# Storing two samples per transfer: one 8 KB run per partition against two rows of 4 KB

## The chip, the cores and the metric

The kernel runs on one core of a Trainium2 chip. The metric is the device time of one execution in microseconds, as the median over runs. Lower is better.

## The reference

There are 128 samples `x[b]` of 128 channels by 1024 time steps in float32, a subject number in 0..7 for each sample, and a table of 8 weight matrices of 128 by 128. Each sample is multiplied by the weights of its subject, and the product is added to it:

```python
w = weights[subjects]
out = jnp.einsum('bct,bcd->bdt', x, w)
x = x + out
```

The input x and the output are 67.1 MB each.

## The kernel before

The 128 samples are taken in 64 groups of two (`G = 2`). A group lives in one of 23 SBUF buffers (`SLOTS = 23`) of 128 partitions by 2 x 1024 floats, so 8 KB per partition and 1 MB per group. The buffers are used in turn. The sum is written over the sample in its buffer, and the buffer is then stored.

- SP issues all the big loads, one of 512 KB per sample, through the helper `transfer` (L53). Each reads runs of 16 KB from HBM (four channels of a sample are contiguous there) and writes one row of 4 KB into each partition. In the first turn SP lets only a few groups be in flight (it waits for the load of three groups earlier); in later turns it waits on `s_store` until the buffer's previous contents have been stored.
- POOL copies the weights of a sample's subject out of `w_all` into one of four buffers (L158).
- PE waits for the load, and multiplies: two matmuls of 512 columns per sample into PSUM (L164), which the profile shows as four records.
- DVE adds the product to the sample, in place (L174), and counts `s_added`.
- ACT waits on `s_added` for both samples of a group and issues one store of 1 MB (also through `transfer`, L53). `s_store` of the buffer tells when it has landed.

Nothing is planned or reordered: each engine runs its own list in the order of the program, and semaphores tie them together. Loads go through SP's DMA queue (q1 in the profile), stores through ACT's (q10). Both queues are served by the same 16 DMA engines. `transfer` builds the DMA instruction itself from both access patterns, so that the two sides may have differently shaped runs; `dma_start` is the language's usual call.

Of the kernel before, what the change touches and what calls it, by code (L numbers as in the profile page):

```python
# [1 line left out]

# [4 lines left out]

F32 = mybir.dt.float32
I32 = mybir.dt.int32
ALU = mybir.AluOpType


G = 2

N = 512  # L30

SLOTS = 23

W_SLOTS = 4
P_SLOTS = 4
DMA = 16

LEAD = 3

IDLE = 3  # L40

ROWS = 4
QUEUES = {mybir.EngineType.SP: "qSPDynamicHW", mybir.EngineType.Activation: "qActDynamicHW"}


def transfer(nc, engine, out, in_):

    later, nc._always_lower_symbolic_ap = nc._always_lower_symbolic_ap, False  # L50
    ins, outs = engine.lower_ap_dma(in_), engine.lower_ap_dma(out)
    nc._always_lower_symbolic_ap = later
    return engine.add_instruction(  # L53
        mybir.InstDMACopy(
            name=nc.get_next_instruction_name(),
            engine=engine.engine,
            ins=ins,
            outs=outs,
            mode="Copy",
            cce_op=ALU.bypass,  # L60
            queue=QUEUES[engine.engine],
        )
    )


@with_exitstack
def kernel(
    ctx: ExitStack,
    tc: tile.TileContext,
    x: bass.AP,  # L70
    subjects: bass.AP,
    weights: bass.AP,
    out: bass.AP,
):
    nc = tc.nc
    B, C, T = x.shape
    S, _, D = weights.shape
    NT = B // G

    def sbuf(name, *shape, dtype=F32):  # L80
        return ctx.enter_context(nc.sbuf_tensor(name, list(shape), dtype)).ap()

    given, near, wrap, index = (
        sbuf(name, 1, B, dtype=I32) for name in ("given", "near", "wrap", "index")
    )
    w_all = sbuf("w_all", C, S, D)
    ws = [sbuf(f"w{i}", C, 1, D) for i in range(W_SLOTS)]
    zeros = sbuf("zeros", C, N)
    xs = [sbuf(f"x{i}", C, G, T) for i in range(SLOTS)]
    ps = [  # L90
        ctx.enter_context(nc.psum_tensor(f"ps{i}", [D, T], F32)).ap() for i in range(P_SLOTS)
    ]

    s_given = tc.alloc_semaphore("s_given")
    s_wall = tc.alloc_semaphore("s_wall")
    s_index = tc.alloc_semaphore("s_index")
    s_zeros = tc.alloc_semaphore("s_zeros")
    s_copied = tc.alloc_semaphore("s_copied")
    s_product = tc.alloc_semaphore("s_product")
    s_added = tc.alloc_semaphore("s_added")  # L100
    s_load = [tc.alloc_semaphore(f"s_load{i}") for i in range(SLOTS)]
    s_store = [tc.alloc_semaphore(f"s_store{i}") for i in range(SLOTS)]

    with tc.tile_critical():  # L104

        nc.scalar.dma_start(given, subjects.rearrange("(o b) -> o b", o=1)).then_inc(s_given, DMA)

        nc.vector.memset(zeros, 0.0).then_inc(s_zeros, 1)  # L108
        nc.tensor.wait_ge(s_zeros, 1)
        for _ in range(IDLE):  # L110
            nc.tensor.matmul(  # L111
                ps[P_SLOTS - 1][:, :N], zeros[:, :D], zeros, start=True, stop=True
            )

        nc.vector.wait_ge(s_given, DMA)
        nc.vector.tensor_scalar(near, given, -S, S - 1, ALU.max, ALU.min).then_inc(s_index, 1)  # L118
        nc.vector.wait_ge(s_index, 1)
        nc.vector.tensor_scalar(wrap, near, 0, S, ALU.is_lt, ALU.mult).then_inc(s_index, 1)  # L120
        nc.vector.wait_ge(s_index, 2)
        nc.vector.tensor_tensor(index, near, wrap, ALU.add).then_inc(s_index, 1)  # L122
        nc.gpsimd.wait_ge(s_index, 3)

        nc.sync.dma_start(w_all, weights.rearrange("s c d -> c s d")).then_inc(s_wall, DMA)  # L127
        for i in range(NT):
            k, turn = i % SLOTS, i // SLOTS
            if turn:  # L130
                nc.sync.wait_ge(s_store[k], DMA * turn)
            elif i >= LEAD:
                nc.sync.wait_ge(s_load[k - LEAD], DMA * G)
            for g in range(G):
                transfer(
                    nc,
                    nc.sync,
                    xs[k][:, g, :],
                    x[i * G + g].rearrange("(a r) t -> a (r t)", r=ROWS),
                ).then_inc(s_load[k], DMA)  # L140

        nc.gpsimd.wait_ge(s_wall, DMA)
        for i in range(NT):
            k, turn = i % SLOTS, i // SLOTS
            nc.tensor.wait_ge(s_load[k], DMA * G * (turn + 1))
            for g in range(G):
                b = i * G + g
                s = nc.values_load(
                    index[0:1, b : b + 1],
                    engines=[mybir.EngineType.Pool],  # L150
                    min_val=0,
                    max_val=S - 1,
                    skip_runtime_bounds_check_because="the index is clamped on the chip above",
                )
                w, p = ws[b % W_SLOTS], ps[b % P_SLOTS]
                if b >= W_SLOTS:
                    nc.gpsimd.wait_ge(s_product, b - W_SLOTS + 1)
                nc.gpsimd.tensor_copy(w, w_all[:, bass.ds(s, 1), :]).then_inc(s_copied, 1)  # L158

                nc.tensor.wait_ge(s_copied, b + 1)  # L160
                if b >= P_SLOTS:
                    nc.tensor.wait_ge(s_added, b - P_SLOTS + 1)
                for t in range(0, T, N):
                    mm = nc.tensor.matmul(  # L164
                        p[:, t : t + N],
                        w[:, 0, :],
                        xs[k][:, g, t : t + N],
                        start=True,
                        stop=True,
                    )  # L170
                mm.then_inc(s_product, 1)

                nc.vector.wait_ge(s_product, b + 1)
                nc.vector.tensor_tensor(xs[k][:, g, :], p, xs[k][:, g, :], ALU.add).then_inc(  # L174
                    s_added, 1
                )
            nc.scalar.wait_ge(s_added, (i + 1) * G)
            transfer(
                nc,
                nc.scalar,  # L180
                out[i * G : (i + 1) * G].rearrange("g d t -> d g t"),
                xs[k].rearrange("d (o g) t -> d o (g t)", o=1),
            ).then_inc(s_store[k], DMA)


        for i in range(NT - SLOTS, NT):
            nc.sync.wait_ge(s_store[i % SLOTS], DMA * (i // SLOTS + 1))


# [1 line left out]
_INS = ["x", "itok_B_0_7", "L0_cond_weights"]  # L191
_OUTS = [((128, 128, 1024), "float32")]


# [20 lines left out]
```

## Time and profile before

| | us |
|---|---|
| median of 3 runs | 327.76 (327.57 to 328.29) |
| the profiled execution | 328.11 |
| its span, first to last instruction | 326.2 |
| PE busy | 239.9 (74%) |
| DVE busy | 157.9 (48%) |
| POOL busy | 37.8 (12%) |

The mean granted TensorE clock is 0.928. HBM traffic is 134.7 MB, 413 GB/s over the span. A line of the form `L164 PE MATMUL` names the line of the kernel, the engine and the operation. In a row of DMA queues stand the packets, the megabytes, and the time that the packets took as a share of the time of 16 engines. In rows of stages, a DMA share slightly above 1 means that the records of neighbouring packets overlap by a few ns.

### The profile page before, as it was taken

The page shows a single profiled execution, that of the slowest core. Times are in us where ns is not written, and L with a number is a line of the kernel's source. Part 1 is how long each engine was busy: PE and PEld are TensorE (multiplying, and loading weights), DVE is VectorE, ACT ScalarE, POOL GpSimd, SP SyncE. Part 2 cuts the span into 40 slices and gives each one's busy share as a digit, 9 for nine tenths or more (in the row PEclk, how much of TensorE's full clock was granted, in tenths as well). Part 3 has the DMA queues.
Part 4 walks back from the last instruction along what each step waited for, and adds up shares of the span by engine and source line. Part 5 has one row for each costly group of instructions (what it writes and reads, how often), then busy time and mean ns, then how long its engine had stood idle before and what let it go on. Part 6 is the DMA issues. An engine that isn't in the chain of part 4 may idle for free.

```text
span 326.2 us, 1941 instructions
## 1 busy us (share of the span) xinstructions
PE 239.9 (74%) x518; PEld 94.5 (29%) x518; DVE 157.9 (48%) x132; POOL 37.8 (12%) x132
## 2 busy tenths in 40 slices
PE   6999989889899998998898898898776866000000
PEld 2444333333333333333333333333232322000000
DVE  1676665565565555665565565666445446000000
POOL 1111111111111111111111111111111110000000
PEclk9999999999999999999999999999999999655555
DMA  7999999999999999999999999999999999999993
GB/s 259 418 415 424 423 420 425 421 430 422 427 424 423 422 426 421 426 424 427 425 425 422 425 427 420 425 424 422 424 432 430 420 422 424 428 424 428 424 428 163
DMA packets 16411, 134.86 MB, mean 413 GB/s; under 512 B 3089, under 2 KB 4114, under 8 KB 4114
## 3 DMA queue, kind: packets, MB, share of 16 engines
q1 hardware_dynamic: 7184, 67.64, 49.5%
q10 hardware_dynamic: 9218, 67.11, 49.1%
q8 instruction: 4, 0.07, 0.1%
q14 instruction: 5, 0.04, 0.0%
HBM read 67.63 MB, written 67.11 MB: 413 GB/s over the span
## 4 chain that ended last, share of the span: by engine, by line
DMA 45%; SPq 24%; another core or an unknown queue 13%; PE 1%; issue 1%; DVE 0%
DMA x<-in_x_dram 30%; SPq L53 23%; DMA out_dram<-x 15%; PE ps L164 1%; DVE x L174 0%; SPq L127 0%; SPq L211 0%; SPq L104 0%
## 5 line engine op out<-in xcount | busy, mean ns | idle before, releaser
L164 PE MATMUL ps<-x,w 128*128 128x512 f32 x512 | 234.7, 604 | 34.2 <-DMA x<-in_x_dram 34.1
L174 DVE TENSOR_TENSOR x<-ps,x 128x1024 f32<-128x1024 f32 x128 | 156.7, 1224 | 117.4 <-PE ps L164 117.4
L164 PEld LDWEIGHTS ps<-x,w 128*128 128x128 f32 x512 | 92.6, 189 | 176.7 <-issue 95.2
L158 POOL COPY w<-w_all 128x128 f32 x128 | 37.6, 294 | 228.3 <-PE ps L164 222.3
L111 PE MATMUL ps<-zeros 128*128 128x512 f32 x6 | 5.2, 1035 | 1.7 <-DVE zeros L108 1.7
L111 PEld LDWEIGHTS ps<-zeros 128*128 128x128 f32 x6 | 1.8, 328 | 3.7 <-issue 2.1
L108 DVE MEMSET zeros<- 128x512 f32 x1 | 0.5, 485 | 1.1 <-SPq L104 1.1
L118 DVE TENSOR_SCALAR near<-given 1x128 int32<-1x128 int32 x1 | 0.2, 215 | 0.6 <-DMA given<-in_itok_B_dram 0.6
L122 DVE CUSTOM_DVE_ANT_0 index<-near,wrap 1x256 uint16<-1x256 uint16 x1 | 0.3, 278 | 0.0
L120 DVE TENSOR_SCALAR wrap<-near 1x128 int32<-1x128 int32 x1 | 0.2, 215 | 0.0
L202 POOL MEMSET const-float32-0.0<- 128x1 f32 x1 | 0.1, 98 | 0.2 <-issue 0.2
L202 POOL MEMSET const-bfloat16-1.0<- 128x1 bf16 x1 | 0.1, 102 | 0.0
L202 POOL MEMSET const-uint8-127<- 128x1 uint8 x1 | 0.1, 102 | 0.0
L202 POOL MEMSET const-float32-1.0<- 128x1 f32 x1 | 0.1, 98 | 0.0
## 6 DMA issues: line engine op xcount, KB each, us to landing
x<-in_x_dram SPq DMA_DIRECT2D x128, 512.0 KB, 12.0
out_dram<-x ACTq DMA_DIRECT2D x64, 1024.0 KB, 40.6
w_all<-in_L_cond_weights_dram SPq DMA_DIRECT2D x1, 512.0 KB, 4.3
given<-in_itok_B_dram ACTq DMA_DIRECT2D x1, 0.5 KB
```

What stands on the lines that cost most here:

```text
L53: return engine.add_instruction(mybir.InstDMACopy(name=nc.get_next_instruction_name(), engine=engine.engine, ins=ins, outs=outs, mode="Cop ...
L108: nc.vector.memset(zeros, 0.0).then_inc(s_zeros, 1)
L111: nc.tensor.matmul(ps[P_SLOTS - 1][:, :N], zeros[:, :D], zeros, start=True, stop=True)
L118: nc.vector.tensor_scalar(near, given, -S, S - 1, ALU.max, ALU.min).then_inc(s_index, 1)
L120: nc.vector.tensor_scalar(wrap, near, 0, S, ALU.is_lt, ALU.mult).then_inc(s_index, 1)
L122: nc.vector.tensor_tensor(index, near, wrap, ALU.add).then_inc(s_index, 1)
L158: nc.gpsimd.tensor_copy(w, w_all[:, bass.ds(s, 1), :]).then_inc(s_copied, 1)
L164: mm = nc.tensor.matmul(p[:, t : t + N], w[:, 0, :], xs[k][:, g, t : t + N], start=True, stop=True,)
L174: nc.vector.tensor_tensor(xs[k][:, g, :], p, xs[k][:, g, :], ALU.add).then_inc(s_added, 1)
L202: nc = _bacc.Bacc("TRN2", target_bir_lowering=False, num_devices=1)
```

## The change

The store is issued with `dma_start` on the buffer as it is, 128 partitions by 2 rows by 1024 floats, where `transfer` had been given the two rows of a partition as one run of 2048 floats. The output side has the same shape in both: per partition two rows of 1024 floats in two samples. Loads are untouched and still go through `transfer`.

```diff
             nc.scalar.wait_ge(s_added, (i + 1) * G)
-            transfer(
-                nc,
-                nc.scalar,
-                out[i * G : (i + 1) * G].rearrange("g d t -> d g t"),
-                xs[k].rearrange("d (o g) t -> d o (g t)", o=1),
+            nc.scalar.dma_start(
+                out[i * G : (i + 1) * G].rearrange("g d t -> d g t"), xs[k]
             ).then_inc(s_store[k], DMA)
```

## The prediction

> **What bounds the kernel now.** I read the page first: the 40 slices, the DMA queues, the groups. Then I asked for sums over stages and for the DMA queues inside single stages.
>
> ```profile
> span 326.2 us, 1941 instructions
> ...
> PE   6999989889899998998898898898776866000000
> ...
> DMA  7999999999999999999999999999999999999993
> GB/s 259 418 415 424 423 420 425 421 430 422 427 424 423 422 426 421 426 424 427 425 425 422 425 427 420 425 424 422 424 432 430 420 422 424 428 424 428 424 428 163
> ...
> q1 hardware_dynamic: 7184, 67.64, 49.5%
> q10 hardware_dynamic: 9218, 67.11, 49.1%
> ...
> x<-in_x_dram SPq DMA_DIRECT2D x128, 512.0 KB, 12.0
> out_dram<-x ACTq DMA_DIRECT2D x64, 1024.0 KB, 40.6
> ```
>
> From the second slice to the last but one the 16 DMA engines are 90% busy or more, at about 424 GB/s; no compute engine is as full. The two queues share that time almost equally. The load queue (q1) has 128 loads of 32 pieces of 16 KB, the 1024 pieces of 512 B of w_all, and the semaphore writes: 128 x (32 + 16) + 1024 + 16 = 7184. The store queue (q10) has 64 x (128 + 16) + 2 = 9218, so a store today is 128 pieces of 8 KB and 16 semaphore writes. PE stops at about 277 us (slice 35 on); the rest is stores alone. So the end is set by the work of the DMA engines, not by a wait of PE, DVE or POOL.
>
> Next, the stages (us; busy time and count of PE, PEld, DVE, POOL; clock; DMA share; GB/s):
>
> ```profile
> 3.30:4.10 0.80, 0.80 (x2) 0.34 (x1) 0.00 (x0) 0.00 (x0) 1.00 1.09 330
> 5.00:16.00 11.00, 9.97 (x22) 4.05 (x21) 4.63 (x4) 2.34 (x8) 1.00 1.01 408
> 20.00:200.00 180.00, 161.81 (x354) 63.83 (x353) 107.86 (x89) 25.84 (x89) 1.00 1.01 424
> 225.00:270.00 45.00, 33.99 (x75) 13.31 (x74) 22.73 (x19) 5.25 (x18) 1.00 1.01 425
> 274.00:318.00 44.00, 1.74 (x5) 0.44 (x3) 2.45 (x2) 0.00 (x0) 0.56 1.01 426
> ```
>
> Row by row: w_all alone in 512 B pieces; 16 KB loads alone; loads and stores mixed while slots are free; mixed while loads wait for slots; stores alone. The queues within the long mixed stage (20 to 200 us), then within the stage of stores alone (274 to 318 us):
>
> ```profile
> DMA packets 8384, 76.39 MB, mean 424 GB/s; under 512 B 1859, under 2 KB 1859, under 8 KB 1859
> ...
> q1 hardware_dynamic: 4191, 45.82, 60.3%
> q10 hardware_dynamic: 4186, 30.49, 40.5%
> ```
>
> ```profile
> DMA packets 2574, 18.75 MB, mean 426 GB/s; under 512 B 285, under 2 KB 285, under 8 KB 285
> ```
>
> In the mixed stage the two queues move equally many packets (4191 and 4186), semaphore writes included, so an engine takes one from each in turn. That explains the bytes: two loads' turns of 16 KB and one semaphore against three stores' turns of which 8 in 9 carry 8 KB is 32 : 21.3 KB, 1.50; measured 45.82 / 30.49 = 1.50.
>
> [...]
>
> **The change part by part.** No compute instruction, wait, semaphore or buffer changes, and no order on any engine: ACT still issues 64 stores of 1 MB after the same waits on s_added, SP the same 128 loads. Only the view of the SBUF side changes: two rows of 4 KB per partition in place of one run of 8 KB. The HBM side was two rows of 4 KB, 512 KB apart, and remains so. The pieces on q10 go from 128 to 256 per store.
>
> *Cost of a piece, the dominating term.* With stores alone, 44 us x 16 engines = 704 engine-us for 2574 - 285 = 2289 pieces: 307.6 ns per 8 KB with its eighth of a semaphore write. That write is 9 ns in the trace's packet records, about 6 without the overlap with its neighbours, so 306.9 ns for the piece. With w_all alone, 330 GB/s is 16 x 512 / 330 = 24.8 ns for 512 B. A straight line through both gives 24.8 + 3584 x (306.9 - 24.8) / 7680 = 156.4 ns for 4 KB, 312.9 for two, against 306.9: 6.0 ns more for every 8 KB. Each engine has 64 x 128 / 16 = 512 such pairs, so +3.1 us. The lower bound comes from doubling at the other end. In the mixed stage 180 x 16 = 2880 engine-us, less 3722 stores at 307.6 ns (1145), less some 1400 load semaphores at 6 ns (8), leave 1727 for 2797 loads: 617 ns for 16 KB, just over twice 306.9. There, halving shows no cost: about -0.6 us if the same slope held to 4 KB[...]. [...] I take 2.4 us[...]; range -0.6 to +3.1.
>
> *Issue on ACT, nothing.* An issue now takes 546 ns at least and 3996 in the median because ACT waits for room; behind it stand only later stores. About 22.5 us from issue to landing at 426 GB/s are 9 stores in flight. If the queue has room for so many pieces, it will hold about half, some 5 MB, still over 11 us of work; that hides the doubled pieces. Without that cover, w_all shows the supply: 1024 pieces issued in 0.44 us and moved at 330 GB/s, 645 pieces per us, where stores alone need 426 GB/s / 4096 B = 104.
>
> *Shares of the queues, a moved stall.* Three load turns still bring 32 KB, three store turns now 3 x 16/17 x 4 = 11.3 KB: ratio 2.9 while both queues are full. Of about 424 GB/s, loads get some 315 and stores 109, in place of 255 and 169. Free slots run out sooner: 24.1 MB of slots, less 5.6 loaded by 16 us, less about 2 in flight, at 315 - 109 = 206 GB/s lasts 80 us, to about 96 us instead of about 210. After that SP's loads wait on s_store for most of the run, and the loads follow the stores at about 212 GB/s each. Both cover the same bytes, and a deep store queue stands behind every stall of SP, so the moved stall costs nothing by itself; loads end near 272 us again, with about 22 MB of stores left. PE's matmul records start 428 ns apart when PE does not wait, four per sample: 1.71 us per 512 KB, 306 GB/s. PE then runs back to back up to 96 us, a little behind the loads, and is late for nobody: stores want only 109 GB/s.
>
> *Sum.* The profiled execution took 328.11 us, its span 326.2, so 1.9 lie around it. Its own sum is 328.11 + 2.4 = 330.5; it stood 0.35 above the median of the runs, so I predict 327.76 + 2.4 = 330.2 us (ratio 1.0073).
>
> **Rivals.** *Not slower: the writes already set the pace.* Each 8 KB piece already writes two rows of 4 KB. If the cost sits in the written rows, reads of 4 KB add nothing: it decides if two 4 KB pieces cost under 1.3 ns more than one of 8 KB (0.66 us / 512). For it: 16 KB loads in four rows cost no less than twice an 8 KB store in two. Against it: 512 B at 24.8 ns, which a pure byte rate would do in 19.2 (306.9 / 16). Time 327.2 to 328.4. *The pieces are joined again* and nothing changes: q10 would stay at 9218 packets, 327.8. Little speaks for it.
>
> *Slower still, by read-heavy mixing.* Loads alone ran at 408 GB/s, mixed at 424. If the first stage, now three-quarters loads, ran at 408, its 80 us x 424 = 34 MB would take 83, +3.1 us on top: 331 to 333.5. Against it: load records that follow only a semaphore write are 617.6 ns, after an 8 KB store 616.7.
>
> *Faster.* Mixed stages run at 424, stores alone at 426. If the new alternation removed that difference over 255 us and the pieces cost nothing, 255 x 2/426 = 1.2 us are gained: 326.6. No row shows a reason for it.
>
> **How the numbers follow.** About 0.2% (0.66 us) is what a measurement of this kernel can tell. Piece cost 0.63; read-heavy mix on top 0.11; writes set the pace or pieces joined 0.19, of which most lands within 0.2%; faster 0.07. So slower 0.74, same 0.17, faster 0.09, a little of the second case falling on the fast side. The range goes from 327.7, which leaves the faster case out, to 332.8, which holds the line's full +3.1 and most of the mixing.
>
> **What would show it.** Right: q10 with 64 x 272 + 2 = 17410 packets; stores alone at 420 to 424 GB/s instead of 426; equal packet counts of both queues before about 96 us with load bytes nearly three times store bytes; PE at 9 in the first dozen slices, lower after. Wrong: holes in the DMA row (the queue starves, a time above the range), stores alone at 426 (no piece cost), or 9218 packets.

## The result, and the profile after

The changed kernel takes 329.49 us in the median of 6 runs (329.04 to 329.70), against 327.74 for the kernel before in the same comparison (327.57 to 328.65). The ratio is 1.0045, with a 95% interval of 1.0030 to 1.0059: slower by 1.75 us, where 2.4 us were forecast. The profiled execution took 329.60 us, its span 327.7.

First the page of the changed kernel: the same rows as before.

```profile
span 327.7 us, 1941 instructions
...
PE   6999999999999997599749875967886887000000
...
DMA  7999999999999999999999999999999999999994
GB/s 262 412 408 425 427 421 424 422 422 426 423 417 414 441 407 424 430 417 424 424 423 426 423 425 429 421 426 421 423 423 439 429 412 417 420 421 422 421 418 161
...
q10 hardware_dynamic: 17410, 67.11, 50.0%
q1 hardware_dynamic: 7184, 67.64, 49.2%
```

The DMA row has no holes, so the end is still set by how much work the 16 engines have. The store queue holds exactly the 17410 packets that pieces of 4 KB make. Its share is 50.0% of 327.7 us, 163.9 us per engine, against 49.1% of 326.2, 160.2: 3.7 us more. The load queue went from 161.5 to 161.2. Part of the growth is counted twice, because the records of neighbouring packets overlap. The store queue of the kernel before, in its stage of stores alone (274 to 318 us), shows by how much:

```profile
q10 hardware_dynamic: 2574, 18.75, 101.4%
```

1.4% of 704 engine-us is 9.9 us over 2574 packets, 3.8 ns each. With 512 more packets per engine, 1.9 us are counted twice. What is left, 3.7 - 0.3 - 1.9 = 1.5 us, agrees with the growth of the span, as far as shares rounded to 0.1% (0.3 us) can tell.

Then the stages: loads alone, the first mixed stage, stores alone.

```profile
5.00:16.00 11.00, 10.11 (x22) 4.04 (x21) 4.50 (x4) 2.37 (x8) 1.00 0.99 398
20.00:90.00 70.00, 70.00 (x164) 30.97 (x163) 49.96 (x41) 12.16 (x41) 1.00 1.01 422
274.00:318.00 44.00, 4.50 (x8) 1.58 (x6) 2.45 (x2) 0.00 (x0) 0.58 1.02 421
```

The queues in the first mixed stage, 20 to 90 us, and the packets of the stage of stores alone, 274 to 318 us:

```profile
DMA packets 4001, 29.57 MB, mean 422 GB/s; under 512 B 778, under 2 KB 778, under 8 KB 2668
...
q1 hardware_dynamic: 1996, 21.79, 73.8%
q10 hardware_dynamic: 2002, 7.74, 27.1%
```

```profile
DMA packets 4802, 18.51 MB, mean 421 GB/s; under 512 B 284, under 2 KB 284, under 8 KB 4802
```

Packets per queue are again equal (1996 and 2002), and the bytes now stand at 21.79 / 7.74 = 2.8. Equal counts alone would also come of several packets taken in a row from each queue. The packet records of the kernel before speak against that: of the 16 KB loads between 20 and 200 us that start 3 to 5 ns before the end of exactly one other record, 2108 follow an 8 KB store, 392 a semaphore write, and none another load. PE is busy for the whole 70 us. In the stage of stores alone, 704 engine-us go to 4802 - 284 = 4518 pieces: 155.8 ns each, so 311.6 ns per 8 KB against 307.6. That is 4.0 ns more for each 8 KB, and over 512 pairs per engine it would be 2.1 us.

### The profile page after: what moved, and what is told of

It is laid out like the page before. It is cut to its first block, busy times and chain, and to the rows that moved or that the text cites. A ratio compares the mean times of both kernels' runs of the same rounds, so it can differ in the third digit from the quotient of the medians.

```text
span 327.7 us, 1941 instructions
## 1 busy us (share of the span) xinstructions
PE 240.4 (73%) x518; PEld 101.0 (31%) x518; DVE 157.9 (48%) x132; POOL 38.1 (12%) x132
## 3 DMA queue, kind: packets, MB, share of 16 engines
q10 hardware_dynamic: 17410, 67.11, 50.0%
## 4 chain that ended last, share of the span: by engine, by line
DMA 60%; another core or an unknown queue 9%; PE 8%; SPq 6%; DVE 1%; ACTq 1%; issue 1%
DMA out_dram<-x 31%; DMA x<-in_x_dram 29%; PE ps L163 8%; SPq L52 5%; DVE x L173 1%; ACTq L177 1%; SPq L126 0%; SPq L207 0%; SPq L103 0%
## 5 line engine op out<-in xcount | busy, mean ns | idle before, releaser
L163 PEld LDWEIGHTS ps<-x,w 128*128 128x128 f32 x512 | 99.1, 197 | 173.0 <-issue 116.9
```

The source lines that it names most:

```text
L163: mm = nc.tensor.matmul(p[:, t : t + N], w[:, 0, :], xs[k][:, g, t : t + N], start=True, stop=True,)
```

## The experiments

Each run was timed beside the kernel before on the same chip; ratios are to that.

**Is it the pieces or the call?** The edit gives `transfer` the buffer as the change gives it to `dma_start`:

```diff
-                xs[k].rearrange("d (o g) t -> d o (g t)", o=1),
+                xs[k],
```

> Stores in rows of 4 KB on the SBUF side, but still issued through transfer. The piece theory (each further piece that an engine reads costs about 4 ns: with stores alone 311.6 ns per 8 KB after the change, 307.6 before): 17410 packets on q10, 421 GB/s with stores alone, about 329.5 us, as the changed kernel. The rival that dma_start itself, another form of the issue, is what costs: 327.8 us, as before, even with 17410 packets.

329.22 us against 328.07, ratio 1.0035 (1.0022 to 1.0049), with this queue on the page:

```profile
q10 hardware_dynamic: 17410, 67.11, 50.0%
q1 hardware_dynamic: 7184, 67.64, 49.2%
```

The packets and the shares are the changed kernel's own, and the intervals overlap. The form of the call is not the cause; cutting the SBUF side into rows of 4 KB alone makes the kernel slower.

**What is read, or what is written?** Three kernels, made from the changed one, issue one store per sample, and cut rows on one side after the other. The edit, shortened, is

```diff
-            nc.scalar.dma_start(<out of the group>, <buffer>).then_inc(s_store[k], DMA)
+            for g in range(G):
+                transfer(
+                    nc, nc.scalar,
+                    out[i * G + g],   # or .rearrange("d (h t) -> d h t", h=2)
+                    xs[k][:, g, :],   # or the same with h=1 (4 KB read) or h=2 (2 KB read)
+                ).then_inc(s_store[k], DMA)
```

and the waits on `s_store` count twice as far.

> One store of 512 KB per sample in place of one of 1 MB per group; 4 KB rows read and written. It is the reference point for the next two. Piece theory: the changed kernel plus 64 more semaphore writes per engine at 6 ns, +0.4 us, so about 329.9 us. If the number of stores had a cost of its own (64 more issues on ACT), above 331.

330.01 us, ratio 1.0059 (1.0046 to 1.0073). That is 0.8 us over the run with one store of 4 KB pieces, where 0.4 were expected. The other 0.4 us was not traced to anything, and lies within the spread of the intervals.

> As the run with one store per sample, but each row of 4 KB is written as two of 2 KB. Piece theory, counting only what is read: unchanged against that run, about 329.9 us. The rival that the written rows set the pace: 1024 more rows per engine; at 2 to 4 ns each +2 to +4 us, 332 to 334 us. If an 8 KB piece in two rows cost what it did because of the rows, this run must be slower.

330.25 us, ratio 1.0066 (1.0053 to 1.0080): 0.24 us for 1024 more written rows per engine, 0.2 ns each, where the rival asked for 2 to 4. The store queue still has the 18434 packets of the run before it, so what is read stayed whole, and the trace gives the written elements of these stores as 2048 bytes:

```profile
q10 hardware_dynamic: 18434, 67.12, 50.2%
```

Written rows are close to free here. The two halves of a row lie side by side in HBM; halves far apart were not tried.

> Rows of 2 KB both read and written, one store per sample: the suspected cost doubled and more. Piece theory: 1024 further pieces per engine at 4 ns, +4.1 us on the run with 4 KB rows, about 334 us, and 33794 packets or more on q10. The rival that the written rows set the pace: as the run that writes 2 KB rows. A theory that the loss comes from the loads' larger share (stores 8:1 by turns): more than that, since loads then get over four fifths of the mixed stage, 335 us or above.

334.62 us, ratio 1.0205 (1.0191 to 1.0219): 4.37 us over the run that differs only in what is read, 4.3 ns for each of 1024 further pieces per engine. The piece theory's 334 held, with the price of the changed kernel's own stage.

```profile
q10 hardware_dynamic: 34818, 67.12, 52.5%
```

The rival that written rows set the pace is out. The theory of the loads' larger share asked for 335 us or above, only 0.4 us from what was measured; this run alone does not put it out. The run with loads of 8 KB, below, says more on it.

The three kernels in one stage, 280 to 316 us, all stores alone, in the order of the text:

```profile
280.00:316.00 36.00, 0.00 (x0) 0.00 (x0) 0.00 (x0) 0.00 (x0) 0.51 1.03 420
```

```profile
280.00:316.00 36.00, 0.00 (x0) 0.00 (x0) 0.49 (x1) 0.00 (x0) 0.56 1.03 418
```

```profile
280.00:316.00 36.00, 0.00 (x0) 0.00 (x0) 0.03 (x1) 0.00 (x0) 0.54 1.04 397
```

420 and 418 GB/s with 4 KB read, 397 with 2 KB read. At 420, 418 and 397 GB/s, 8 KB take 312, 314 and 330 ns. So in this stage each of two further written rows costs under 1 ns, and each of two further read pieces 8 ns, more than the run as a whole shows. In the mixed stages a read piece costs less. From 20 to 270 us, the run that writes 2 KB rows and the run that also reads them moved

```profile
DMA packets 17910, 105.35 MB, mean 421 GB/s; under 512 B 3218, under 2 KB 3218, under 8 KB 14231
```

```profile
DMA packets 28616, 104.49 MB, mean 418 GB/s; under 512 B 3193, under 2 KB 3193, under 8 KB 24957
```

That is 0.82% less, 2.0 us of work, for some 680 further pieces per engine: an estimate of 3 ns each. Why the price differs by stage was not tried.

**Do the loads' larger share and the earlier stall for buffers cost anything?** The first attempt leaves the stores alone and makes the loads' turns larger:

```diff
-ROWS = 4
+ROWS = 8
```

> The kernel before with loads in runs of 32 KB and stores in 8 KB pieces: the queues' shares shift towards loads (2.25 to 1 by turns, against 1.50 before and 2.83 after the change), with no smaller piece anywhere. Piece theory: 128 fewer load pieces per engine at 4 ns, 0.5 us less, about 327.2 us. The rival that the shifted shares and the earlier stall for slots cost the time: slower than before, 328.3 to 329.5 us.

It settled nothing on the shares: 397.12 us in the median, single runs from 381 to 423, the shortest still 53 us over the kernel before. The page is of a run of 421.55 us, one of the two longest, so its figures are high for the others. It shows another effect:

```profile
DMA packets 14363, 134.86 MB, mean 321 GB/s; under 512 B 3089, under 2 KB 4114, under 8 KB 4114
...
q1 hardware_dynamic: 5136, 67.64, 56.3%
q10 hardware_dynamic: 9218, 67.11, 42.4%
```

With half the load packets, the load queue takes 56.3% of 419.6 us, 236 us per engine instead of 161. In the packet records a 32 KB load takes 1821 ns in the mean, where two of 16 KB took 1238. The reason was not found.

The second attempt leaves the pieces alone and takes buffers away, so that loads stall for them earlier:

```diff
-SLOTS = 23
+SLOTS = 12
```

> The kernel before with 12 buffers instead of 23: loads run out of free buffers after about 75 us instead of 210, with pieces unchanged. If an earlier stall for buffers costs nothing while the store queue stays deep: 327.8 us, no change. The rival that the stall has a price: 1 us or more, 329 us or above.

328.36 against 328.00 us, ratio 1.0009 (1.0001 to 1.0017): 0.3 us, by the interval at most 0.6, for a stall that begins in the first third of the run. The same edit in the changed kernel:

> The changed kernel with 12 buffers instead of 23: the shift of the shares meets half the buffers, so loads stall for buffers after about 35 us instead of 100. If the earlier stall is free here too (with 8 KB pieces 12 buffers cost 0.3 us): 329.5 to 329.9 us. If the loads' lead is what pays for the stall in the changed kernel: above 330.5 us.

329.43 us, ratio 1.0044 (1.0031 to 1.0057), the ratio of the changed kernel with 23 buffers. So the moved stall costs some tenths of a us at most in the one, and nothing that shows in the other.

**Do loads pay for smaller pieces too?** The changed kernel with `ROWS = 2`, loads in runs of 8 KB:

> The changed kernel with loads in runs of 8 KB: by turns 1.74 to 1, near the shares of before, with more small pieces. Piece theory: 256 more load pieces per engine at 4 ns, +1.0 us, about 330.5 us. The rival that the shares cost the time: back towards the time of before, 328 us.

328.98 us, ratio 1.0030 (1.0019 to 1.0041). The expected +1.0 us is not there. The 8192 load packets of 8 KB fill 49.6% of 326.9 us:

```profile
q10 hardware_dynamic: 17410, 67.11, 50.0%
q1 hardware_dynamic: 11280, 67.64, 49.6%
```

That is 162.1 us per engine, 0.9 more than the 161.2 with 16 KB, and about the 1.0 us that 256 more overlaps of 3.8 ns add to the sum. Loads pay nothing for halving 16 KB. The run also bears on the shares. From 20 to 90 us its queues held

```profile
q1 hardware_dynamic: 2844, 18.67, 63.4%
q10 hardware_dynamic: 2840, 10.97, 38.2%
```

The bytes stand at 1.70, near the 1.50 of the kernel before, and yet the kernel is 1.0 us slower than that one. So the larger share of the loads can explain at most a part of the loss. Whether this version is faster than the changed kernel by some tenths, the intervals don't tell.

The two edits with loads in smaller runs and the old stores, `ROWS = 2` and `ROWS = 1` in the kernel before:

> The kernel before (stores in 8 KB pieces) with loads in runs of 8 KB: loads' and stores' turns now bring about 0.9 to 1, so loads get less than stores would and are never far ahead. The changed kernel with such loads took 328.98 us, so loads pay nothing for 8 KB pieces. If only the stores' pieces count: 327.6 to 328.0 us, and the difference to the changed kernel with 8 KB loads, 1.0 to 1.4 us, is the store pieces' cost with the loads' own cost the same in both. If load pieces cost 4 ns as the stores' do: +1 us, 329.0 us.

331.05 us, ratio 1.0093 (1.0079 to 1.0107), which is 2 us more than even the rival expected, and not for the rival's reason. The page:

```profile
PE   6999676776867668767988676786786686677771
...
DMA  6999999999999999999999999999999999999964
GB/s 238 414 420 426 425 425 422 425 426 425 425 426 424 425 423 426 423 424 425 423 423 427 427 423 425 423 426 423 426 427 424 424 426 424 421 426 427 424 273 175
```

The rate in the middle is 421 to 427 GB/s, as before the change. The loss is in the last two slices: 273 and 175 GB/s, where the kernel before had 428 and 163. With pieces of 8 KB on both queues, loads are no longer ahead: from 20 to 270 us they moved 52.57 MB and the stores 53.57, where the kernel before had 61.01 and 45.01. The packet records have the last load landing at 317.7 us instead of 271.5, and matmuls, adds and stores of the last samples follow it while the DMA engines run empty.

> The kernel before with loads in runs of 4 KB: 768 more load pieces per engine than in runs of 16 KB. If a piece costs 4 ns on either queue: +3.1 us, 331 us. [...] Here the loads get the smaller share (0.46 to 1 by turns), so the stores wait for loads and stores alone at the end nearly vanish; if loads alone, at 408 GB/s, then fill the gaps, +1 us or more without any cost of a piece.

333.08 us, ratio 1.0179 (1.0148 to 1.0209). Two things lie on top of each other here. The last load lands at 318.8 us, as in the run just told, and the pieces of the loads now have a price. From 20 to 270 us, well before the end, the runs with loads in 8 KB and in 4 KB moved

```profile
DMA packets 15383, 106.23 MB, mean 425 GB/s; under 512 B 2420, under 2 KB 2420, under 8 KB 2420
```

```profile
DMA packets 21733, 105.53 MB, mean 422 GB/s; under 512 B 2425, under 2 KB 2425, under 8 KB 15284
```

That is 0.66% less, 1.65 us of work, for some 400 further load pieces per engine: about 4 ns each, an estimate from one profile of either run. Loads that pay nothing for halving 16 KB do pay for halving 8 KB.

**Larger pieces.** If 4 KB pieces cost, 16 KB ones might gain. Groups of four samples in 11 buffers:

```diff
-G = 2
+G = 4
-SLOTS = 23
+SLOTS = 11
-LEAD = 3
+LEAD = 2
```

> Groups of four samples in 11 buffers of 16 KB per partition (two groups of loads in flight in the first turn): a store is 2 MB and reads 16 KB pieces. Piece theory, carried on to larger pieces: 256 fewer store pieces per engine at 4 ns and 32 fewer semaphore writes, 1.2 us less than before, about 326.6 us. The rival that coarser groups cost more than they save (the first store some 3 us later, loads alone at 408 GB/s, and a last store of twice the size): 327.8 us or more.

333.77 us, ratio 1.0173 (1.0135 to 1.0212): the rival's side, and by far more than it asked. The page:

```profile
DMA  7999999999999999999999999999999999999655
GB/s 255 412 410 426 428 421 430 420 436 416 434 422 427 424 426 430 414 429 421 428 428 418 434 416 432 422 430 424 428 424 416 433 424 422 424 430 426 289 224 253
...
q1 hardware_dynamic: 7184, 67.64, 49.0%
q10 hardware_dynamic: 4610, 67.11, 47.8%
```

The store queue's work did shrink, from 160.2 to 158.2 us per engine, though half of that is the double count of 256 overlaps. The last three slices lost it: 289, 224 and 253 GB/s, since the last loads land at 313.9 us and nothing is left in the store queue to fill the time until the last group is done. None of the kernels tried beats the kernel before.

## Why the prediction was right

**The mechanism.** DMA work sets the end, and the change adds to it by pieces. Shown from three sides: the same packets by another call give the same time, 1024 further read pieces per engine cost 4.37 us, and 1024 further written rows cost 0.24. The issue on ACT, put at nothing, added nothing: one took 3565 ns in the median, 3996 before.

**The size.** This term was too large: 2.4 us, where the medians differ by 1.75 and the interval of the ratio allows 1.0 to 1.9. The point was the author's estimate below the line's 3.1 us; no trace shows why it should lie there. The line missed: 6.0 ns more for each 8 KB, where the stage of stores alone measured 4.0. Its lower point was 0.8 us of w_all in 512 B pieces. Whether it misled because those are loads and not stores, or because so short a stretch says little, is open.

The lower end of the range, -0.6 us, missed as well, and no single price for a piece fits the runs. A further piece cost nothing when 16 KB loads were halved (162.1 us per engine against 161.2, no more than the added overlaps), about 4 ns when 8 KB loads were, and in stores of 2 KB pieces 3 ns in the mixed stages and 8 with stores alone.

The 4.0 ns do not hold for the whole run either; they would make 2.1 us. From 20 to 270 us the kernel before moved 106.12 MB, the changed one 105.90 and the run with the same packets by `transfer` 105.79. That is 0.5 to 0.8 us of work for some 346 pairs per engine, an estimate of 1.5 to 2.2 ns for each 8 KB. With 4.0 ns for the 166 pairs left to the stage of stores alone, the sum is 1.2 to 1.4 us, near the 1.5 us that the span grew. In the packet records a 16 KB load takes 617.7 ns in the mean after the change and 619.2 before, 0.4 us over 256 loads. The cause of that was not tested, and it may be scatter: in the two runs that read 4 KB and write 4 or 2 KB rows, it took 618.3 and 621.2 ns, while their times were 0.24 us apart.

**The shares.** One packet from each queue in turn held: 2.9 was forecast, 2.8 measured, and equal packet counts lasted until between 100 and 105 us, where 96 was forecast. The rate of loads by the view is 21.79 MB / 70 us = 311 GB/s against 315, of stores 111 against 109. PE ran back to back, as expected, though to about 130 us (slice 16). The last load landed at 272.6 us, with 272 forecast. That the moved stall costs nothing was argued in the prediction; the two runs with 12 buffers show that it costs some tenths of a us at most. The cover it named, a deep store queue behind every stall, agrees with the two runs whose loads landed late and that were slower: 331.05 us with the last load at 317.7, and 333.77 with the last at 313.9.

**The queue depth** was wrong, without consequence. That ACT waits for room agrees with the packed trace of the kernel before: the first 17 issues took 546 to 637 ns, with at most eight stores on the way when one was issued, and from the point at which nine were on the way, an issue took 2.0 to 9.2 us. How much fits was not halved by the smaller pieces: after the change, stores took 17.4 us from issue to landing in the stage of stores alone; at 421 GB/s that is 7.3 MB in flight, not the 5 MB of a limit counted in read pieces.

**The rivals.** Joined pieces: out, by 17410 packets. Writes set the pace: out, by the run that cut the written rows alone and cost 0.24 us. Read-heavy mixing: the first mixed stage ran at 422 GB/s, not 408. The faster case had no part: stores alone fell to 421.

## What to carry to other kernels

In this kernel the DMA engines are 90% busy or more in all but the first and the last slice, and the time grows with what the pieces cost: 4.37 us for 1024 further read pieces per engine. A piece of a store is counted on the side that is read (18434 packets with 4 KB read and 2 KB written, 34818 with 2 KB read), so hand a store the 8 KB run that its source has, even if the destination has to be cut: that was worth 0.5% here. Going on to larger pieces is not shown to help. Stores of 16 KB saved about 1 us of the queue's work and lost more at the end (333.77 us), and loads of 32 KB were much slower (397.12 us).

When two queues share engines packet by packet, the piece sizes also decide who runs ahead, here 1.50 to 2.8 bytes loaded for one stored. Keep the loads ahead, so that stores are left to fill the end. A change that costs little per byte can cost more by losing that lead, as loads of 8 KB did in the kernel before (331.05 us against 327.98, at an unchanged rate in the middle), so read the last slices before the mean rate.

## What the runs showed that was not expected

- Load pieces of 32 KB: 1821 ns in place of twice 619, and 381 to 423 us for the kernel. In a store, a piece of 16 KB took 617 ns in the packet records, close to twice the 312 of 8 KB.
- Loads in 8 KB runs cost no more than in 16 KB, but in 4 KB runs about 4 ns for each further piece. The price of a piece differed with its size and with the stage: in stores of 2 KB pieces 3 ns in the mixed stages, 8 with stores alone.
- Both queues at 8 KB pieces cost 3.1 us against the kernel before, at an unchanged rate in the middle: the loss is the end alone.
